# The head of a gated S4 and feed-forward kernel: the order of the first requests, the root of block 0, and two sums cut differently

## The chip, the cores and the metric

The kernel runs on one core of one Trainium2 chip. The metric is device time in microseconds (us) of one execution; the median of three runs of the kernel before is 442.58 us. All arithmetic is in float32.

## The reference

The input `x` has 2 x 1024 rows of 512 numbers. Cut to what matters:

```python
xn = layernorm(x)                                   # over the 512 numbers of a row, eps 1e-5
s  = causal_convolution(xn, K) + D * xn             # K: a kernel of length 512 from an S4 state space
h1 = xn @ w1.T + 2 * (xn @ A1.T) @ B1.T             # w1, w3: 1376 x 512, LoRA rank 16
h3 = xn @ w3.T + 2 * (xn @ A3.T) @ B3.T
g  = silu(h1) * h3
y  = g @ w2.T + 2 * (g @ A2.T) @ B2.T               # w2: 512 x 1376
out = x + s * silu(y)
```

## The kernel before

**Tiling.** The 2048 rows are four blocks of 512 rows (0 to 3), each of four tiles of 128 rows. Blocks 0 and 1 form the first superblock, 2 and 3 the second. The 1376 hidden units are five pairs of 128-wide chunks and a last chunk of 96, for `w1` and for `w3`. The LoRA terms are merged into the weights on the chip: a product of rank 16 on TensorE (PE), then `merge` adds twice that to the weight tile on VectorE (DVE, line 393).

**Products.** The two big products use Strassen's scheme in Winograd's form, with seven products and some sums of operands in place of eight products. It is applied twice for the pairs: an outer level over rows (b11, b21, b12, b22) and weights, an inner level within these. So each pair has seven chains (1, 2, 6, 7, 5, 3, 4), one for each outer product, and each chain has seven steps, one for each inner product. The last chunk has one chain for each superblock. A step is a product into a PSUM bank on PE (line 756) and often a copy of that bank by ScalarE (ACT: lines 776, 794) or an addition by DVE (lines 780, 870) that frees the bank. The PSUM has two banks for each of the tags x, y, w and aux; `bank(tag)` takes the next of a tag, `bank(tag, True)` borrows it without moving on.

**Sums of operands.** `outer_token_sum` (L328) and `inner_token_sum` (L341 for name 3, L343 for name 2, L345 for 4, L347 for 1) make the token sums, `outer_weight_sums` (L441) and `inner_weight_sum` (L453) those of the weights, all on DVE. An inner token sum is made for the raw tokens (`xr`, three parts of 512 columns, `raw` true) and for the outer sums (`xt`, four parts), as one instruction or two. GpSimd (POOL) takes over some additions (L870) and the product of the gate (L837), after which SP stores the result to `g_dram` (L808).

**Head.** `load_x` requests a block's tiles. Block 0 comes over the SP and the ACT queue; block 1 goes to single tiles; blocks 2 and 3 to free room in `t_in`. The DMA requests of SP and ACT share eight semaphores in turn, so each request waits until the one eight places before it has landed. Each block is normalized: statistics (`norm_stats`, L247 and L248, on DVE), the reciprocal root (`norm_root`: L281, `rsqrt` with L57 to L66, then L284), the normalization itself (`normalize`: ACT L293, POOL L297), and the transposition by PE (L304), whose result ACT copies (L312; for blocks 1 and 3 L314 and L315). Block 3's statistics are made by ACT (L254, L265). `keep_warm` gives PE idle products (L991) while it waits for data.

**LoRA groups.** The rank-16 factors lie in rows 0 to 15 of each quarter of the partitions: groups 0 and 1 hold those of `w1` and `w3`, groups 2 and 3 a second copy of both. `lora_last` uses groups 0 and 1. `merge_pair`, used for pair 0, makes the product of half a pair from groups 0 and 1, and is called twice; `merge_whole_pair`, used for pairs 1 to 4, uses all four groups at once and gives four merges.

**Order.** PE, DVE, ACT and POOL run in the order in which the program emits instructions. That order is set by hand: `at(place, what)` puts a piece of work at a number, pieces are emitted in rising order of these numbers, and `after(delay, what)` adds one at a distance from the piece that is being emitted. A chain's step is placed by tables such as `PLACES`; one step of a pair's chain is worth about one unit. The code up to `pair_chain` runs first, then the places from -11 on. SP takes the requests as they are emitted.

Of the kernel before, what the change touches and what calls it, by code (L numbers as in the profile page):

```python
# [49 lines left out]
def rsqrt(nc, pool, v, shape):  # L50


    y = pool.tile(shape, F32, tag="rs_y", name="rs_y")
    t = pool.tile(shape, F32, tag="rs_t", name="rs_t")
    part = 3.0 / 8.0
    c2 = part * 0.703952253
    nc.vector.tensor_scalar(  # L57
        y.bitcast(I32), v.bitcast(I32), -0.5, float(0x5F1FFFF9), ALU.mult, ALU.add
    )
    nc.vector.tensor_tensor(t, y, y, ALU.mult)  # L60
    nc.vector.scalar_tensor_tensor(t, t, -c2, v, ALU.mult, ALU.mult)
    nc.vector.scalar_tensor_tensor(y, t, c2 * 2.38924456, y, ALU.add, ALU.mult)
    nc.vector.tensor_tensor(t, y, y, ALU.mult)
    nc.vector.scalar_tensor_tensor(t, t, 1.0 / part**2, v, ALU.mult, ALU.mult)
    nc.vector.scalar_tensor_tensor(t, t, -10.0 / 3.0, t, ALU.add, ALU.mult)
    nc.vector.scalar_tensor_tensor(y, t, 5.0, y, ALU.add, ALU.mult)  # L66
    return y
# [40 lines left out]
def s4_gated_ffn(  # L108
# [59 lines left out]
    def bank(tag, borrow=False):  # L168

        i = turn[tag]  # L170
        if not borrow:
            turn[tag] = 1 - i
        return psum.tile([P, 512], F32, tag=f"{tag}{i}", name=tag, bufs=1)
# [36 lines left out]
    def value(tag="s"):  # L210
        return upool.tile([P, TB], F32, tag=tag, name=tag, bufs={"s": 10, "c": 4}[tag])
# [4 lines left out]
    def at(place, what):  # L216
        heapq.heappush(events, (place, next(count), what))

    def after(delay, what):
        at(now[0] + delay, what)  # L220
# [2 lines left out]


    def load_x(b):
        room = (None, None, t_in[4], t_in[6])[b]
        tiles = []
        for tt in range(NTT):
            t = value() if room is None else room[:, tt, :]
            queue = nc.scalar if b == 0 and tt % 2 else nc.sync  # L230
            queue.dma_start(out=t, in_=x[bass.ds(b * TB + tt * P, P), :])
            tiles.append(t)
        return tiles

    norms, sums_of_x = {}, {}

# [38 lines left out]
            norms[b][:, :, 1], sums_of_x[b][:, 2, :], 1.0 / DIM, None, mult  # L275
        )

    def norm_root(mv, *blocks):
        n = len(blocks) * NTT
        veps = small.tile([P, n], F32, tag="veps", name="veps")  # L280
        nc.vector.tensor_scalar(veps, mv[:, :, 1], EPS, None, add)  # L281
        rstd = rsqrt(nc, small, veps, [P, n])
        shift = small.tile([P, n], F32, tag="shift", name="shift")
        nc.vector.scalar_tensor_tensor(shift, mv[:, :, 0], -1.0, rstd, mult, mult)  # L284
        for n, b in enumerate(blocks):
            norms[b] = [t[:, n * NTT : (n + 1) * NTT] for t in (rstd, shift)]
# [9 lines left out]
            else:  # L296
                nc.gpsimd.tensor_scalar(t, t, rstd[:, one], shift[:, one], mult, add)  # L297

    def transpose(b, tiles, tag="aux"):
        sb, low = divmod(b, 2)  # L300
        for tt in tiles:
            ps = bank(tag)
            for dc in range(NDC):
                nc.tensor.transpose(  # L304
                    ps[:, dc * P : (dc + 1) * P],
                    x_in[b][tt][:, dc * P : (dc + 1) * P],
                    ident,
                )
            at_ = slice(tt * P, (tt + 1) * P)
            halves = ps.rearrange("p (c k t) -> p c k t", c=2, k=2)  # L310
            if low == 0:
                nc.scalar.copy(xr[:, 0:2, sb, :, at_], halves)  # L312
            else:
                nc.scalar.copy(b12[sb][:, :, at_], halves[:, 0])  # L314
                nc.scalar.copy(xr[:, 2, sb, :, at_], halves[:, 1])  # L315
# [18 lines left out]

    def inner_token_sum(name, raw, half=None):
        src, lo, n = (xr, 0, 3) if raw else (xt, 3, 4)
        some = slice(n) if half is None else slice(2 * half, 2 * half + 2)
        to = {i: t[:, lo : lo + n, :][:, some] for i, t in t_in.items()}
        b11, b21, b12_, b22 = (src[:, some, s, k, :] for s in range(2) for k in range(2))
        if name == 3:  # L340
            nc.vector.tensor_tensor(to[7], b22, b12_, sub)  # L341
        elif name == 2:
            nc.vector.tensor_tensor(to[6], to[7], b11, add)  # L343
        elif name == 4:
            nc.vector.tensor_tensor(to[4], b21, to[6], sub)  # L345
        else:
            nc.vector.tensor_tensor(b12_, b12_, b11, sub)  # L347
# [21 lines left out]
    def load_lora(queue, group, d, h, lo, hi):  # L369
        rows = slice(32 * group, 32 * group + R)  # L370
        if d is not None:
            queue.dma_start(out=lora["d"][rows, :], in_=d)
        queue.dma_start(out=lora["h"][rows, : hi - lo], in_=h[:, lo:hi])
        lora["base"][group] = lo
# [6 lines left out]
    def lora_product(ps, group, dc, lo, n, start=True):  # L381
        d, h = lora_factors(group, lo, n)
        nc.tensor.matmul(
            ps,
            lhsT=d[:, dc * P : (dc + 1) * P],
            rhs=h,
            start=start,
            stop=True,
            skip_group_check=True,
        )  # L390

    def merge(to, ps):
        nc.vector.scalar_tensor_tensor(to, ps, LORA_SCALE, to, mult, add)
# [11 lines left out]
                )  # L405
        return w

    def merge_pair(c, w, half, tag="aux"):

        ps = [bank(tag), bank(tag)]  # L410
        for k in range(2):
            for v in range(2):
                n = slice(k * 2 * P, (k + 1) * 2 * P)
                lora_product(ps[v][:, n], v, 2 * half + k, PAIR_AT[c], 2 * P, k == 0)
        for v in range(2):
            to = w[:, (1, 2, 0, 3)[2 * v + half]].rearrange("p k m h -> p (k m h)")
            after(1.6 + v, lambda to=to, v=v: merge(to, ps[v]))

    def merge_whole_pair(c, w, first=None, delays=(1.15, 2.3, 4.3, 4.4)):

        ps = [first or [bank("y", True), bank("w", True)], [bank("aux"), bank("aux")]]
# [41 lines left out]
    def load_last():  # L463
        both = const.tile([P, 2, 2 * NDC * LASTR], F32, tag="w2b", name="last")
        w, s = (
            both[:, i].rearrange("p (a b h) -> p a b h", a=n, h=LASTR)
            for i, n in enumerate((2, 4))
        )
        for v, src in enumerate((w1T, w3T)):
            nc.sync.dma_start(  # L470
                out=w[:, v], in_=src[:, LAST * P :].rearrange("(dc p) h -> p dc h", p=P)
            )
        return w, s

    def lora_last():
        ps = [bank("y"), bank("y")]
# [487 lines left out]

    x_in = {0: load_x(0)}
    warm = const.tile([P, 1], F32, name="warm")
    nc.gpsimd.memset(warm, 0.0)
    make_identity(nc, ident)
    lora_tiles(LSPLIT)
    factors = (a1, b1T), (a3, b3T)  # L970
    for v, f in enumerate(factors):
        load_lora((nc.sync, nc.scalar)[v], v, *f, LSPLIT, HID)
    nc.scalar.activation(warm, warm, AF.Silu)
    x_in[1] = load_x(1)
    make_upper_triangular(nc, tri, 1.0, diag=True)
    w_last, s_last = load_last()
    w_pair, s_pair = {0: load_pair(0)}, {c: {} for c in range(NPAIR)}
    x_in[2], x_in[3] = load_x(2), load_x(3)
    w_pair[1] = load_pair(1)
    for v, f in enumerate(factors):  # L980
        load_lora(nc.sync, 2 + v, *f, LSPLIT, HID)

    def other_factors():
        for v, (_, h) in enumerate(factors):
# [18 lines left out]
    ps_last = lora_last()  # L1003
    mv = norm_tile(0)
    norm_stats(0, range(NTT))
    norm_root(mv, 0)
    normalize(0)

    keep_warm(primed[1], 4)
    transpose(0, range(NTT))  # L1010
    mv = norm_tile(1)
    norm_stats(1, range(2))
    merge_last(w_last, ps_last, 0)
    norm_stats(1, range(2, NTT))
    norm_root(mv, 1)
    merge_last(w_last, ps_last, 1)
    mv_late = norm_tile(2, 3)
    ab_last = last_operands(w_last, s_last)

# [37 lines left out]
            add_chain(2 + 7 * c + n, pair_chain(c, n), places)  # L1057
    at(-10, lambda: normalize(1))
    at(-9.9, lambda: last_sums(w_last, s_last))
    at(-9, lambda: merge_pair(0, w_pair[0], 0))  # L1060
    at(-3.8, lambda: merge_pair(0, w_pair[0], 1))
    for i in range(2):
        at(-6 + i, lambda i=i: transpose(1, range(2 * i, 2 * i + 2), "y"))
    for n, name in enumerate((3, 2, 1)):
        at((-2.3, -1.5, -0.45)[n], lambda name=name: outer_token_sum(0, name))
        at(-0.6 + 0.3 * n, lambda name=name: outer_weight_sums(w_pair[0], (name,)))
    at(0.4, lambda: outer_token_sum(0, 4))
    at(0.8, lambda: outer_weight_sums(w_pair[0], (4,)))
    for tt in range(NTT):
        at(-6 + 0.8 * tt, lambda tt=tt: norm_stats(2, (tt,)))  # L1070
        at(-1.4 + 0.1 * tt, lambda tt=tt: act_sums(3, tt))
        at((-0.3, -0.2, 1.7, 1.8)[tt], lambda tt=tt: act_squares(3, tt))
    at(-0.9, lambda: act_means(3))
    at(1.9, lambda: act_variances(3))
    at(6.9, lambda: norm_root(mv_late, 2, 3))
    at(7.3, lambda: normalize(2))
    at(7.7, lambda: normalize(3, (0,)))
    for n, place in enumerate((12.1, 12.8, 13.7, 14.4)):
        b, i = divmod(n, 2)
        at(place, lambda b=b, i=i: transpose(2 + b, range(2 * i, 2 * i + 2)))  # L1080
# [5 lines left out]
        at(when, lambda name=name: inner_weight_sum(w_pair[0], s_pair[0], name))  # L1086
    for name, raw, when, *half in (
        (3, True, 21.6),
        (2, True, 22.8),
        (3, False, 24.2),  # L1090
        (2, False, 30.2),
        (1, True, 34.4),
        (1, False, 37.5, 0),
        (1, False, 40.3, 1),
        (4, True, 47.6),
        (4, False, 50.2, 0),
        (4, False, 52.3, 1),
    ):
        at(when, lambda of=(name, raw, *half): inner_token_sum(*of))
# [495 lines left out]
```

## Time and profile before

| | |
|---|---|
| median of three runs | 442.58 us (442.12, 442.58, 443.27) |
| the profiled execution | 442.84 us |
| its span, first to last instruction | 441.0 us |
| granted clock of PE | 0.998 of full speed |
| busy: PE, DVE, POOL, ACT | 434.3, 317.6, 207.9, 144.3 us |
| moved by DMA | 53.61 MB, mean 122 GB/s |

The page gives the busy time of each engine and the chain that ended last; other views list the same execution by stretches or in order of time. In a line of the timeline the columns are start and duration in us, engine, line of the kernel, operation, output<-inputs by tile name, shapes, and count; a bracket gives the idle time of the engine before it and what ended that. PE is the product, PEld the load of its weights. The time of a run is longer than the span by what lies around the first and the last instruction (here 1.8 us).

### The profile page before, as it was taken

How to read it: one execution, taken by the hardware profiler on the slowest of the kernel's cores; microseconds unless marked ns; L12 is line 12 of the kernel's file. 1: busy time of each engine (PE TensorE's matmuls, PEld its weight loads, DVE VectorE, ACT ScalarE, POOL GpSimd, SP SyncE). 2: the span in 40 equal slices, each digit the busy share in tenths (PEclk: the TensorE clock that was granted, in tenths of full speed). 3: DMA queues.
4: the chain of work that ended last, by engine and by line, in shares of the span. 5: the costliest groups of instructions: out<-in, count | busy, mean ns of one | idle time of the engine just before them, and what ended most of it. 6: DMA issues, size and time to landing. Idle time of an engine off the chain costs nothing.

```text
span 441.0 us, 5158 instructions
## 1 busy us (share of the span) xinstructions
PE 434.3 (98%) x1704; PEld 269.1 (61%) x1704; DVE 317.6 (72%) x536; ACT 144.3 (33%) x296; POOL 207.9 (47%) x156
## 2 busy tenths in 40 slices
PE   7999999999999999999999999999999999999996
PEld 7645334344444444444443446888898999999996
DVE  5899999954974687469745796979786885653234
ACT  2777242453255324532453242211101212212221
POOL 1416468895689368946894468400000122222221
PEclk9999999999999999999999999999999999999999
DMA  8931304025102500250035526395901832422211
GB/s 242 364 83 44 124 0 149 10 84 159 36 24 80 159 24 25 88 170 25 25 129 206 162 94 214 94 364 189 344 33 71 296 129 95 144 97 95 77 67 48
DMA packets 35467, 53.61 MB, mean 122 GB/s; under 512 B 4689, under 2 KB 21521, under 8 KB 35313
## 3 DMA queue, kind: packets, MB, share of 16 engines
q1 hardware_dynamic: 35088, 52.69, 36.3%
q10 hardware_dynamic: 352, 0.60, 0.4%
q8 instruction: 13, 0.21, 0.2%
q14 instruction: 14, 0.11, 0.1%
HBM read 33.88 MB, written 19.40 MB: 121 GB/s over the span
## 4 chain that ended last, share of the span: by engine, by line
PE 86%; DVE 7%; DMA 2%; ACT 2%; issue 1%; POOL 0%; SPq 0%; DVEq 0%; ACTq 0%; POOLq 0%
PE x L756 43%; PE y L756 22%; PE w L756 11%; PE aux L930 4%; PE w L930 2%; DMA s<-in_x_dram 1%; DVE xt L328 1%; DVE s L453 1%; DVE w L441 1%; DMA w<-in_w1T_dram 1%; PE y L529 1%; PE aux L711 1%; DVE t_in L343 1%; ACT c L254 1%; DVE aux L1310 1%
## 5 line engine op out<-in xcount | busy, mean ns | idle before, releaser
L1313 POOL TENSOR_TENSOR o<-o,xin 128x512 f32<-128x512 f32 (+1 forms) x17 | 23.3, 1369 | 133.0 <-DVE o L1312 133.0
L837 POOL TENSOR_TENSOR s<-c,s 128x512 f32<-128x512 f32 (+1 forms) x44 | 63.2, 1442 | 17.6 <-ACT c L829 12.4
L776 ACT COPY s<-x 128x512 f32<-128x512 f32 (+1 forms) x54 | 31.5, 584 | 84.5 <-PE x L756 84.4
L756 PE MATMUL x<-t_in,s 128*128 128x512 f32 (+1 forms) x148 | 55.4, 501 | 0.0
L870 POOL TENSOR_TENSOR s<-ua_three,s 128x512 f32<-128x512 f32 x20 | 35.9, 1793 | 25.4 <-DVE s L780 25.4
L780 DVE TENSOR_TENSOR s<-s,y 128x512 f32<-128x512 f32 (+1 forms) x54 | 36.0, 679 | 15.7 <-PE y L756 10.6
L756 PEld LDWEIGHTS x<-t_in,s 128*128 128x128 f32 x148 | 26.6, 190 | 23.3 <-issue 11.7
L870 POOL TENSOR_TENSOR ua_three<-ua_three,s 128x512 f32<-128x512 f32 x20 | 30.6, 1529 | 13.8 <-DVE s L780 13.8
L756 PE MATMUL y<-t_in,s 128*128 128x256 f32 (+1 forms) x108 | 35.9, 459 | 0.1
L1335 ACT COPY z<-x 128x256 f32<-128x256 f32 x24 | 8.8, 371 | 70.5 <-PE x L756 70.4
L870 POOL TENSOR_TENSOR s<-u_three,s 128x512 f32<-128x512 f32 x20 | 29.4, 1474 | 1.8 <-ACT c L829 1.0
L1310 DVE TENSOR_TENSOR aux<-aux,m 128x384 f32<-128x384 f32 x32 | 18.1, 565 | 15.8 <-PE aux L930 14.3
L829 ACT ACTIVATE c<-c 128x512 f32<-128x512 f32 x40 | 25.2, 632 | 12.9 <-DVE c L870 12.9
L756 PEld LDWEIGHTS y<-t_in,s 128*128 128x128 f32 x108 | 20.1, 190 | 11.6 <-issue 8.1
L794 ACT COPY w<-x 128x512 f32<-128x512 f32 (+1 forms) x37 | 21.1, 570 | 11.6 <-PE x L756 11.5
L870 POOL TENSOR_TENSOR u_three<-ua_three,u_three 128x512 f32<-128x512 f32 x10 | 15.6, 1556 | 13.4 <-DVE u_three L780 13.3
L756 PE MATMUL x<-t_in,w 128*128 128x512 f32 x40 | 21.0, 605 | 0.0
L756 PE MATMUL x<-xt,w 128*128 128x512 f32 x40 | 20.7, 598 | 0.0
L756 PE MATMUL x<-xr,w 128*128 128x512 f32 x40 | 20.6, 614 | 0.0
L756 PE MATMUL x<-xr,s 128*128 128x512 f32 x40 | 20.5, 614 | 0.0
L756 PE MATMUL x<-xt,s 128*128 128x512 f32 x40 | 20.4, 592 | 0.0
L756 PE MATMUL y<-xt,w 128*128 128x512 f32 x40 | 19.8, 592 | 0.0
(302 smaller groups left out, 908.7 us busy)
## 6 DMA issues: line engine op xcount, KB each, us to landing
g_dram<-s SPq DMA_DIRECT2D x40, 256.0 KB, 2.1
g<-g_dram SPq DMA_DIRECT2D x10, 512.0 KB, 5.8
xin<-in_x_dram SPq DMA_DIRECT2D x16, 256.0 KB, 2.7
out_dram<-o SPq DMA_DIRECT2D x14, 256.0 KB, 2.0
t_in<-g_dram SPq DMA_DIRECT2D x6, 512.0 KB, 4.1
w<-in_w1T_dram SPq DMA_DIRECT2D x10, 256.0 KB, 3.6
w<-in_w3T_dram SPq DMA_DIRECT2D x10, 256.0 KB, 4.9
t_in<-in_x_dram SPq DMA_DIRECT2D x8, 256.0 KB, 5.7
```

The source lines that it names most:

```text
L254: nc.scalar.activation(value("c"), x_in[b][tt], AF.Copy, accum_out=sums_of_x[b][:, 0, tt : tt + 1])
L756: nc.tensor.matmul(ps[:, cols], lhsT=lhsT, rhs=rhs if parts == 1 else rhs[:, cols], start=first and i == 0 and part == 0, stop=i == len(pa ...
L776: nc.scalar.copy(t, self.x)
L780: nc.vector.tensor_tensor(t, t, self.y, add)
L794: nc.scalar.copy(self.w, self.x)
L829: nc.scalar.activation(c, c if src is None else src, AF.Silu)
L837: nc.gpsimd.tensor_tensor(g, act, g, mult)
L870: (nc.vector if o < 20 else nc.gpsimd).tensor_tensor(to, a, b, add)
L930: nc.tensor.matmul(to[:, n * P : (n + 1) * P], lhsT=x_, rhs=by, start=start, stop=True, skip_group_check=True,)
L1310: nc.vector.tensor_tensor(y[:, P:], y[:, P:], m[:, n * P : (n + 3) * P], add)
L1313: (nc.vector if last else nc.gpsimd).tensor_tensor(o, o, self.xin[h][:, cols], add)
L1335: nc.scalar.copy(t, xb)
```

## The change

- Block 1 is loaded into `t_in[7]` by two requests of 512 KB in place of four of 256 KB; blocks 2 and 3 likewise into their rooms.
- The second copy of the LoRA factors (groups 2 and 3) is requested right after the weights of the last chunk, ahead of pair 0, blocks 2 and 3 and pair 1; before, it came behind them. The weights of the last chunk are now requested ahead of the POOL work on `tri`.
- Block 0's reciprocal root: ACT takes the root (`Sqrt`), DVE the reciprocal and one step of refinement. The first activation loads the table for Sqrt; a second warm-up activation after block 0's transposes loads the one for Silu.
- Block 0's transposes use the banks aux, aux, x, aux; block 1's use x (borrowed) and y, y, y. One warm-up product of PE less.
- Pair 0's LoRA is made by `merge_whole_pair`, once, with the banks y, y, aux, aux, and its four merges stand together; `merge_pair` is gone. The second merge of the last chunk moves ahead of block 1's root.
- The statistics of three tiles of block 2 move from -5.2, -4.4 and -3.6 to 0.84, 0.85 and 0.9; its normalization from 7.3 to 7.7.
- The inner token sum of name 2 (T2) is made in four instructions in place of two.

```diff
     def load_x(b):
...
+        if b == 0:
+            tiles = [value() for _ in range(NTT)]
+            for tt, t in enumerate(tiles):
+                (nc.sync, nc.scalar)[tt % 2].dma_start(out=t, in_=x[bass.ds(tt * P, P), :])
+            return tiles
+        room = (None, t_in[7], t_in[4], t_in[6])[b]
+        for tt in range(0, NTT, 2):
+            nc.sync.dma_start(
+                out=room[:, tt : tt + 2, :],
+                in_=x[bass.ds(b * TB + tt * P, 2 * P), :].rearrange("(n p) d -> p n d", p=P),
+            )
+        return [room[:, tt, :] for tt in range(NTT)]
...
+    def refined(mv, veps):
+
+        shape = list(veps.shape)
+        y = small.tile(shape, F32, tag="rs_y", name="rs_y")
+        t = small.tile(shape, F32, tag="rs_t", name="rs_t")
+        root = small.tile(shape, F32, tag="root", name="root", bufs=1)
+        nc.scalar.activation(root, mv[:, :, 1], AF.Sqrt, bias=eps)
+        nc.vector.tensor_scalar(veps, mv[:, :, 1], EPS, None, add)
+        nc.vector.reciprocal(y, root)
+        nc.vector.tensor_tensor(t, y, y, mult)
+        nc.vector.scalar_tensor_tensor(t, t, -0.5, veps, mult, mult)
+        nc.vector.scalar_tensor_tensor(y, t, 1.5, y, add, mult)
+        return y
...
+        if on_act:
+            rstd = refined(mv, veps)
+        else:
+            nc.vector.tensor_scalar(veps, mv[:, :, 1], EPS, None, add)
+            rstd = rsqrt(nc, small, veps, [P, n])
...
-        some = slice(n) if half is None else slice(2 * half, 2 * half + 2)
+        some = slice(n) if half is None else slice(2 * half, min(2 * half + 2, n))
...
-    nc.scalar.activation(warm, warm, AF.Silu)
+    nc.scalar.activation(warm, warm, AF.Sqrt)
     x_in[1] = load_x(1)
+    w_last, s_last, load_of_last = load_last()
+    for v in range(2):
+        load_of_last(v)
     make_upper_triangular(nc, tri, 1.0, diag=True)
-    w_last, s_last = load_last()
+    for v, f in enumerate(factors):
+        load_lora(nc.sync, 2 + v, *f, LSPLIT, HID)
     w_pair, s_pair = {0: load_pair(0)}, {c: {} for c in range(NPAIR)}
     x_in[2], x_in[3] = load_x(2), load_x(3)
     w_pair[1] = load_pair(1)
-    for v, f in enumerate(factors):
-        load_lora(nc.sync, 2 + v, *f, LSPLIT, HID)
...
-    norm_root(mv, 0)
+    norm_root(mv, 0, on_act=True)
     normalize(0)
 
-    keep_warm(primed[1], 4)
-    transpose(0, range(NTT))
+    keep_warm(primed[1], 3)
+    for tt, tag in enumerate(("aux", "aux", "x", "aux")):
+        transpose(0, (tt,), tag)
+    nc.scalar.activation(warm, warm, AF.Silu)
     mv = norm_tile(1)
     norm_stats(1, range(2))
     merge_last(w_last, ps_last, 0)
     norm_stats(1, range(2, NTT))
+    merge_last(w_last, ps_last, 1)
     norm_root(mv, 1)
-    merge_last(w_last, ps_last, 1)
...
-    at(-9, lambda: merge_pair(0, w_pair[0], 0))
-    at(-3.8, lambda: merge_pair(0, w_pair[0], 1))
-    for i in range(2):
-        at(-6 + i, lambda i=i: transpose(1, range(2 * i, 2 * i + 2), "y"))
+    at(
+        -9,
+        lambda: merge_whole_pair(
+            0, w_pair[0], [bank("y"), bank("y")], (1.6, 1.7, 1.8, 1.9)
+        ),
+    )
+    at(-6, lambda: transpose(1, (0,), "x", True))
+    at(-5.9, lambda: transpose(1, range(1, NTT), "y"))
...
-        at(-6 + 0.8 * tt, lambda tt=tt: norm_stats(2, (tt,)))
+        at((-6, 0.84, 0.85, 0.9)[tt], lambda tt=tt: norm_stats(2, (tt,)))
...
-    at(7.3, lambda: normalize(2))
-    at(7.7, lambda: normalize(3, (0,)))
+    at(7.7, lambda: normalize(2))
+    at(7.75, lambda: normalize(3, (0,)))
...
         (3, True, 21.6),
-        (2, True, 22.8),
+        (2, True, 22.8, 0),
         (3, False, 24.2),
-        (2, False, 30.2),
+        (2, False, 30.2, 0),
+        (2, False, 30.3, 1),
+        (2, True, 31.1, 1),
         (1, True, 34.4),
```

More of the change, by code (lines that the diff above doesn't have):

```diff
@@ L225, in load_x @@
     def load_x(b):
[L226 to L233, printed above, removed]
+        if b == 0:
[10 more added lines that the diff above has]
+        return [room[:, tt, :] for tt in range(NTT)]
     norms, sums_of_x = {}, {}
@@ L276, in act_variances, with norm_root @@
         )
-    def norm_root(mv, *blocks):
+    def refined(mv, veps):
[10 more added lines that the diff above has]
+        return y
+    def norm_root(mv, *blocks, on_act=False):
         n = len(blocks) * NTT
         veps = small.tile([P, n], F32, tag="veps", name="veps")
-        nc.vector.tensor_scalar(veps, mv[:, :, 1], EPS, None, add)
-        rstd = rsqrt(nc, small, veps, [P, n])
+        if on_act:
[3 more added lines that the diff above has]
+            rstd = rsqrt(nc, small, veps, [P, n])
         shift = small.tile([P, n], F32, tag="shift", name="shift")
@@ L297, in normalize, with transpose @@
                 nc.gpsimd.tensor_scalar(t, t, rstd[:, one], shift[:, one], mult, add)
-    def transpose(b, tiles, tag="aux"):
+    def transpose(b, tiles, tag="aux", borrow=False):
         sb, low = divmod(b, 2)
         for tt in tiles:
-            ps = bank(tag)
+            ps = bank(tag, borrow)
             for dc in range(NDC):
@@ L406, in load_pair @@
         return w
[L408 to L417, printed above, removed]
     def merge_whole_pair(c, w, first=None, delays=(1.15, 2.3, 4.3, 4.4)):
@@ L468, in load_last, with load @@
         )
-        for v, src in enumerate((w1T, w3T)):
+        def load(v):
             nc.sync.dma_start(
-                out=w[:, v], in_=src[:, LAST * P :].rearrange("(dc p) h -> p dc h", p=P)
+                out=w[:, v],
+                in_=(w1T, w3T)[v][:, LAST * P :].rearrange("(dc p) h -> p dc h", p=P),
             )
-        return w, s
+        return w, s, load
     def lora_last():
@@ L966, in s4_gated_ffn @@
     warm = const.tile([P, 1], F32, name="warm")
-    nc.gpsimd.memset(warm, 0.0)
+    eps = const.tile([P, 1], F32, name="eps")
+    for t, v in ((warm, 0.0), (eps, EPS)):
+        nc.gpsimd.memset(t, v)
     make_identity(nc, ident)
```

## The prediction

> **What bounds the kernel now.** I read the chain that ended last first, its shares by engine:
>
> ```profile
> PE 86%; DVE 7%; DMA 2%; ACT 2%; issue 1%; POOL 0%; SPq 0%; DVEq 0%; ACTq 0%; POOLq 0%
> ```
>
> PE carries 86% of the chain, and followed in order of time its other pieces lie in the first 62 us, but for single spots. So I took the stretches of 10 us (columns: length, then busy PE, PEld, DVE, ACT and POOL, granted clock, DMA share, GB/s):
>
> ```profile
> 20.00:30.00 10.00, 10.00 (x33) 4.31 (x32) 9.33 (x17) 8.92 (x25) 1.06 (x3) 1.00 0.52 157
> 50.00:60.00 10.00, 9.94 (x24) 3.61 (x23) 9.90 (x9) 3.25 (x6) 4.91 (x2) 1.00 0.00 0
> 70.00:80.00 10.00, 10.00 (x25) 4.24 (x24) 9.97 (x11) 3.82 (x7) 7.56 (x5) 1.00 0.41 126
> 90.00:100.00 10.00, 10.00 (x24) 4.23 (x24) 4.66 (x7) 5.04 (x9) 9.69 (x8) 1.00 0.24 79
> ```
>
> PE and DVE are both full from 20 to 90 us; only after 90 has DVE room (4.66 of 10). An earlier start of PE is therefore worth what DVE, equally full, can follow. The timeline shows where the two meet:
>
> ```profile
> 8.17 0.17 DVE L281 TENSOR_SCALAR veps<-mv 128x4 f32<-128x4 f32 x1
> 10.14 1.52 ACT L293 ACTIVATE s<-s,shift,rs_y 128x512 f32<-128x512 f32 x2 [6.07 <-DVE shift L284]
> 12.34 1.21 PE L304 MATMUL aux<-ident,s 128*128 128x128 f32 x8 [0.24 <-ACT xr L312]
> 15.37 0.56 ACT L794 COPY w<-x 96x512 f32<-96x512 f32 x1 [1.19 <-PE x L756]
> 21.47 1.13 PE L383 MATMUL aux<-lo_h,lo_d 16*128 16x256 f32 x8
> 21.55 1.29 DVE L328 TENSOR_TENSOR xt<-xr,b 128x512 f32<-128x512 f32 x2 [0.64 <-ACT xr L315]
> ...
> 52.79 2.64 DVE L343 TENSOR_TENSOR t_in<-t_in,xr 128x1536 f32<-128x1536 f32 x1
> 55.35 0.67 DVE L870 TENSOR_TENSOR c<-ua_one,x 128x512 f32<-128x512 f32 x1
> 69.31 2.95 DVE L347 TENSOR_TENSOR xt<-xt 128x1024 f32<-128x1024 f32 x1
> 81.91 0.68 DVE L870 TENSOR_TENSOR c<-u_one,x 128x512 f32<-128x512 f32 x1
> 82.64 0.30 PEld L756 LDWEIGHTS x<-t_in,w 128*128 128x128 f32 x2 [0.75 <-DVE c L870]
> ```
>
> Until 21.5 us a chain of small steps sets the pace. DVE's last long wait is the 0.64 before 21.55; from there it runs almost without a break to 92, and PE waits for it at 56 (behind the row of 55.35) and at 82.64 (behind that of 81.91).
>
> **Root from Sqrt.** Removed is DVE's row of ten small instructions (L281, L57 to L66, L284), 8.17 to 10.11. In its place stand Sqrt on ACT, then reciprocal, three small operations and the shift; veps runs beside Sqrt. The last statistics end at 8.13. Two hand-overs of 0.04; Sqrt of 128x4 by its nearest row, the 128x1 ACTIVATE at 3.88 us, 0.20; reciprocal 0.18 (128x4, L669); four more at the 0.196 spacing of L57 to L66: 9.4, or 0.7 earlier. At 0.8 for Sqrt (L293, 128x512 with pointer operands) only 0.1 earlier.
>
> **Transposes in a third bank.** The wait at 12.34 (0.4 with its refill) goes, and ACT copies four tiles in a row at 0.48 (L312). Its two normalizations last from 9.4 to 10.95, the copies to 13.0 instead of 14.2. The warm-up matmul less ran while PE waited anyway: nothing.
>
> **Second table load.** After the copies ACT loads the table for Silu. The load at 2.58 us took 1.28, the ACTIVATE behind it 0.20: ACT is taken to 14.5, and behind it waits the copy L794 that opens the last chunk's second product; it goes at 14.55 (before: 15.37). The LoRA products hide this, just: PE has them from 14.0 to 15.1, then needs the copy. Without that cover it costs 0.4. The Trainium skill, "ScalarE: Activation LUTs", section "What ACT_TABLE_LOAD costs", adds about 1.38 us of drain to every switch of the table. The load in this trace shows none (its ACTIVATE follows 0.01 later); by the page the copy would go at 15.9, and the sum below would be 0.4 slower instead of 0.4 faster.
>
> **LoRA four at a time.** Before, two sets of L383 stand in PE's row, 1.06 each (15.26 and 21.47); four row groups together took 1.08 at 30.48. PE is relieved of 1.06. On DVE four merges (L393, 0.60 each) stand together behind the root of block 1, where two did: those of 22.76 and 24.56 come forward. The first two banks are those of the last chunk's LoRA, so PE also waits for the second L393 on `last`, which now stands ahead of block 1's root and delays it by its 0.6. DVE starts block 1's statistics 0.7 earlier, waits some 0.4 for the first `last` piece, and ends the root near 15.9 as now (15.78).
>
> **Factors and block 1.** The moved factor requests pass the first pair, blocks 2 and 3 and the second pair on SP. SP's thirteenth to sixteenth requests went out at 7.43 to 9.02; these are now the factors. The two `last` transfers took 3.7 and 4.7 us, landing near 11.1 and 12.6; DMA is full there (share 1.02 to 1.08), so sending them 1 us earlier brings nothing, and the factors follow at some 0.2 each: 13.4. PE asks at 14.0. High end: 9.02 and the longest landing of lo_d, 6.4, give 15.4. The first pair lands 0.7 later, near 16.3; DVE's merges run from 15.9 to 18.3, so they wait little. Blocks 2 and 3 land 0.7 later too; their statistics come later than before, and ACT's sums have over 1 us of room. Block 1 in two requests moves the same bytes: nothing, 0.3 either way.
>
> **Sum to 21 us.** The last chunk's second product goes at 15.15 instead of 16.32; block 1's transposes at 16.9 instead of 18.11 (normalized at 16.8, so no earlier). Over three banks only the fourth tile waits, 0.6 for ACT. The last copy is done at 20.1 instead of 21.5: DVE's L328 starts 1.35 earlier, and PE, one LoRA set lighter, is 1.6 earlier.
>
> **What DVE makes of it.** From L328 on it is 1.35 earlier; two merges gone, 1.2 more; three tiles' statistics of block 2 (L247 with L248, 0.80 each) now stand behind the sums, 2.4 back; waits of 0.11 and 0.24 (30.1, 34.2) close, as ACT is ahead. That leaves 0.5 at the merges of 34.8. **T2 in four parts** (L343): the row of 52.79 becomes two thirds, 0.53 less (L341: 2.28 for 2048, 1.74 for 1536), so DVE is 1.0 ahead at 55.35. The row of 59.34 becomes two halves, 0.06 more, and PE's next product needs only the first. The last third costs 0.60 some 2 us later: 0.4 ahead is left, and at 82 PE waits for DVE as before. The later place of the normalizations (7.7 for 7.3) costs nothing: it lets a ready copy pass the late root. The sum: 0.4 earlier. Against the profiled execution's own 442.84 (span 441.0, 1.8 around it) that is 442.4; the median of the runs, 442.58, is 0.26 lower: **442.2 us**.
>
> **Rivals.** First, *the whole head start survives* (faster). DVE's row from 63 to 76 us holds waits: L347 of 1024 takes 1.69 at 65.89 and 2.95 at 69.31, L345 of the same size 1.21 at 82.51; with the rows of 1536 at 63.15 and 75.28 it is some 3.2 us, always with POOL on SBUF beside it. If the new order meets POOL 1 us less, DVE no longer holds PE; 1.35 to 1.6 remain, and the stalls at 56 and 82 (up to 0.5) may go: 440.5 to 441.2. Second, *the split opens DVE to POOL* (slower): while DVE works back to back on SBUF, POOL's L870 at 48.69 takes 5.12; it gets in at a break, and DVE then loses 0.5 to 1.7 (65.89, 69.31). Four parts for two make two more breaks, 1.0 to 3.4; less the 0.4, 443.2 to 445.6. It decides once DVE loses over 0.4 more between 52 and 74 us. Against it: POOL's work is the same and gets in somewhere anyway. Third, *the factors do not come first*: eight requests stood ahead already and still do (block 0, groups 0 and 1); landing at 15.4, they hold PE 1.4: 443.6.
>
> **How the numbers follow.** Forecast 0.45, first rival 0.33, second 0.14, third 0.08. About 0.3%, 1.3 us, is what a measurement of this kernel can tell from no change; the forecast and the third rival lie within it almost whole, the first rival beyond it, the second mostly. Faster 0.36, same 0.49, slower 0.15. The forecast's own range is 441.3 to 443.0 (Sqrt at its long end, one meeting with POOL more or less); to leave out no more than 2 in 10 it must reach through the first rival and into the second: 440.5 to 443.9.
>
> **What would show it.** Right: normalization at 9.4, the second table load ended by 14.6, one L383 set near 14.0 and none at 21, L328 near 20.2, DVE full from there to 91, and the stall at 82 still behind L870. Wrong: DVE idle before 80 us (first rival), more L343 or L347 rows above 2 us (second), L383 waiting for lo_h after 14.5 (third), or a stall that no row of before has.

## The result, and the profile after

| | before | changed |
|---|---|---|
| median of 20 runs each | 442.16 us (441.69 to 443.27) | 444.49 us (442.62 to 446.57) |
| ratio, 95% interval | | 1.0047 [1.0035, 1.0059] |
| the profiled execution, its span | 442.84, 441.0 | 444.26, 442.5 |

The change makes the kernel slower, by 2.3 us of the median. Two things stand out in the times alone. The changed kernel's runs spread over 4 us, those of before over 1.6. And six of its 20 runs show a granted clock of 0.992 to 0.995 and take 445.5 to 446.6 us; the other fourteen are at 0.997 to 1.000. The profiled execution is none of the six, so this profile shows only a part of the loss.

The chain that ended last, shares by engine (it could be followed back only to 49 us, so they can't be set beside those of before):

```profile
PE 79%; DVE 6%; DMA 2%; issue 0%; ACT 0%; DVEq 0%; SPq 0%
```

The same stretches as before (columns as there):

```profile
20.00:30.00 10.00, 9.31 (x32) 3.64 (x34) 9.29 (x17) 8.96 (x24) 1.16 (x4) 1.00 0.54 191
50.00:60.00 10.00, 9.93 (x24) 3.59 (x23) 9.91 (x10) 2.92 (x6) 5.44 (x2) 1.00 0.00 0
70.00:80.00 10.00, 10.00 (x25) 4.22 (x24) 8.96 (x11) 3.44 (x6) 9.84 (x6) 1.00 0.48 138
90.00:100.00 10.00, 10.00 (x24) 4.07 (x23) 4.95 (x8) 5.60 (x10) 9.69 (x8) 1.00 0.22 79
```

PE now waits in the first stretch, and from 70 to 80 POOL has 2.3 us more (9.84 for 7.56) and DVE 1.0 less: DVE there waits for PE, which had waited for DVE just before. The timeline (lines 328, 343, 347, 383, 453, 756, 794, 837 and 870 of before are now 349, 364, 368, 404, 463, 769, 807, 850 and 883):

```profile
7.42 0.17 DVE L289 TENSOR_SCALAR veps<-mv 128x4 f32<-128x4 f32 x1
7.48 0.30 ACT L288 ACTIVATE root<-mv,eps 128x4 f32<-128x4 f32 x1 [3.40 <-DVE mv L252]
8.81 1.52 ACT L314 ACTIVATE s<-s,shift,rs_y 128x512 f32<-128x512 f32 x2 [1.03 <-DVE shift L305]
11.63 0.56 DVE L414 SCALAR_TENSOR_TENSOR last<-y,last 128x384 f32<-128x384 f32 x1 [0.99 <-DMA last<-in_w1T_dram]
12.44 1.28 ACT L1029 ACT_TABLE_LOAD   x1
13.74 0.20 ACT L1029 ACTIVATE warm<-warm 128x1 f32<-128x1 f32 x1
14.27 0.56 ACT L807 COPY w<-x 96x512 f32<-96x512 f32 x1 [0.33 <-PE x L769]
20.64 1.29 DVE L349 TENSOR_TENSOR xt<-xr,b 128x512 f32<-128x512 f32 x2 [1.29 <-ACT xr L336]
...
61.02 1.08 DVE L463 TENSOR_TENSOR s<-w 128x896 f32<-128x896 f32 x1
62.02 1.76 DVE L364 TENSOR_TENSOR t_in<-t_in,xr 128x512 f32<-128x512 f32 x1
63.70 0.67 DVE L883 TENSOR_TENSOR ua_one<-ua_one,w 128x512 f32<-128x512 f32 x1
64.30 1.74 DVE L368 TENSOR_TENSOR xr<-xr 128x1536 f32<-128x1536 f32 x1
69.51 1.13 PE L769 MATMUL x<-xr,s 128*128 128x512 f32 x2 [0.49 <-DVE ua_one L883]
69.98 1.21 DVE L368 TENSOR_TENSOR xt<-xt 128x1024 f32<-128x1024 f32 x1
74.11 0.69 DVE L883 TENSOR_TENSOR ua_one<-ua_one,w 128x512 f32<-128x512 f32 x1 [1.03 <-PE w L769]
83.28 1.13 PE L769 MATMUL x<-t_in,w 128*128 128x512 f32 x2 [0.54 <-DVE c L883]
238.88 1.12 PE L769 MATMUL y<-t_in,s 128*128 128x512 f32 x2 [0.54 <-DVE w_a L414]
```

The fourth piece of T2 at 62.02 is a sum over 512 columns; free, that takes 0.68 (so in the profile of the kernel with the statistics between the sums, below). It took 1.76, and the next instruction on DVE starts 1.15 later than before. At 69 us DVE is still 0.67 late, and PE waits for it at 69.51. The sum behind, at 69.98, then runs without POOL beside it and takes 1.21, where the one of before took 2.95 at 69.31. DVE would be 1.0 ahead, but now it has to wait 1.03 for PE, at 74.11. Two further sums beside POOL (at 75.31, 2.43 for 2.29, and at 78.26, 1.56 for 1.08) put it behind again, and PE waits a second time at 83.28, where it is 0.64 later than before. Counted from start to start of products, beyond their usual spacing, the two stalls are 0.66 and 0.71. In the kernel before, the stall at this second place is 0.09: the 0.75 in its row of 82.64 is idle time of the weight load, not of PE. The wait at 238.88, 0.54 in its row and 0.70 counted from start to start, is for a merge of `w2` whose transfer landed at 238.04, 1.2 us later than in the profile of before. Such waits come and go: in the profiles of the kernels below the same place shows nothing in ten, and 0.23 to 0.71 in four.

### The profile page after: what moved, and what is told of

Same layout as the page of the kernel before. It is cut to its first block, busy times and chain, and to the rows that moved or that the text cites. A ratio compares the mean times of both kernels' runs of the same rounds, so it can differ in the third digit from the quotient of the medians.

```text
span 442.5 us, 5158 instructions
## 1 busy us (share of the span) xinstructions
PE 433.1 (98%) x1702; PEld 268.1 (61%) x1702; DVE 315.6 (71%) x534; ACT 146.0 (33%) x299; POOL 213.5 (48%) x157
## 4 chain that ended last, share of the span: by engine, by line
PE 79%; DVE 6%; DMA 2%; issue 0%; ACT 0%; DVEq 0%; SPq 0%
PE x L769 40%; PE y L769 21%; PE w L769 10%; PE aux L943 4%; PE w L943 2%; DMA w_a<-in_w2T_dram 2%; DVE t_in L364 1%; DVE t_in L362 1%; PE y L404 1%; PE aux L724 1%; DVE s L793 1%; DVE aux L1335 1%; DVE ua_one L883 0%; DVE xt L349 0%; DVE o L1337 0%; DVE xr L368 0%
## 5 line engine op out<-in xcount | busy, mean ns | idle before, releaser
L850 POOL TENSOR_TENSOR s<-c,s 128x512 f32<-128x512 f32 (+1 forms) x44 | 66.9, 1527 | 14.6 <-ACT c L842 12.2
L883 POOL TENSOR_TENSOR ua_three<-ua_three,s 128x512 f32<-128x512 f32 x20 | 31.1, 1556 | 12.4 <-DVE s L793 12.4
L807 ACT COPY w<-x 128x512 f32<-128x512 f32 (+1 forms) x37 | 21.1, 571 | 10.7 <-PE x L769 10.6
L769 PE MATMUL y<-xt,s 128*128 128x512 f32 x40 | 19.8, 592 | 0.0
```

The source lines that it names most:

```text
L769: nc.tensor.matmul(ps[:, cols], lhsT=lhsT, rhs=rhs if parts == 1 else rhs[:, cols], start=first and i == 0 and part == 0, stop=i == len(pa ...
L807: nc.scalar.copy(self.w, self.x)
L850: nc.gpsimd.tensor_tensor(g, act, g, mult)
L883: (nc.vector if o < 20 else nc.gpsimd).tensor_tensor(to, a, b, add)
```

## The experiments

All are compared with runs of the kernel before on the same chip; the ratio is to these. Theory A: the cut of T2 meets POOL. Theory B: it costs nothing, transfers do. Theory C came from the first four profiles: POOL's small operation L264 is locked out. Theory D: late transfers make the spread.

**T2 again in two** (the changed kernel, `(2, True, 22.8)` and `(2, False, 30.2)` in place of four lines).

> The changed kernel with T2 again in two instructions; all else of the change stays. Theory A (the fourth piece of T2 meets POOL: it took 1.76 us at 62.02 where 0.67 is free, and DVE then reaches the additions that PE waits for at 69.5 and 83.3 late): those two stalls, 0.66 and 0.71 us, fall to 0.1 to 0.2, and the time is 0.6 us below the changed kernel's 444.5, 443.9 or less. Theory B (the cut of T2 costs nothing; what was lost, was lost to transfers such as that of w2, whose landing held PE 0.70 at 238.9): within 0.3 us of 444.5, with a late stall again near 83.

Ratio 1.0031 [1.0013, 1.0049], median 443.95, spread 441.67 to 446.26. The stalls at 69 and 83 are gone, as theory A says, but the profiled execution took 446.26: PE waited 2.67 us at 31.1 (from start to start of products, beyond their spacing; 2.51 as idle time), a stall that neither of the first two profiles has.

**Only T2 in four** (the kernel before with these four lines).

> The kernel before with only T2 in four instructions. Theory A: the fourth piece stands behind the same inner weight sum, near 62.6, POOL gets in there, the piece takes 1.7 us, and PE waits behind DVE at 82 by 0.6 more: 442.8 or more against 442.16 before. Theory B: the two halves relieve DVE at 55 by 0.5 as forecast and the late piece gives it back: within 0.3 us of before.

Ratio 0.9994 [0.9983, 1.0005]; spread 441.76 to 443.28, as narrow as before. The piece took 1.77 and PE waited 0.59 and 0.71 behind it, just as A says, yet the time did not rise: this profile's head was 0.73 earlier by its landings, and the runs can't tell the rest from nothing. What it does show is that the spread comes with the head, not with T2.

**The fourth piece later, and one statistic back in the head** (`31.1` to `34.3`; `(-6, -5.2, 0.84, 0.85)`).

> The changed kernel with the fourth piece of T2 moved from 31.1 to 34.3, so behind the addition L883 that reads PSUM, which then stands at 62.0, where POOL gets in. Theory A: that addition runs in 0.67 beside POOL, the piece behind it loses 0.5 at most, DVE is 0.6 us earlier at 64, PE's stall of 0.66 at 69.5 falls to 0.1: 0.6 below the changed kernel's 444.5. Theory B: within 0.3 us of it.

> The changed kernel with the statistics of the second tile of block 2 back at -5.2, into the 1.29 us that DVE idles ahead of 20.64. DVE's row from 30 to 52 us becomes 0.8 shorter. If DVE's order is what holds PE (theory A), it is up to 0.8 us ahead at 57 and the stalls at 69.5 and 83.3 shrink by as much: 443.7 to 444.2 where POOL is met as often. If DVE's place in the row is not what counts (theory B): within 0.3 of 444.5.

1.0040 [1.0020, 1.0060] and 1.0037 [1.0016, 1.0059], medians 444.32 and 444.61: neither moved the time clear of noise, against theory A's figures. In the first, the piece took 1.16 and the sum behind it 2.82 where 1.74 to 2.23 was usual: the meeting with POOL moved on by one instruction. In the second, the profiled execution again had the wait of 2.67, at 29.6, and a low clock.

The two profiles with that wait gave theory C. ACT's squares of block 3 need the means that POOL makes (L264 and L265, 128x4 each). In the profile of before POOL makes them beside a merge, which reads PSUM:

```profile
24.56 0.68 DVE L393 SCALAR_TENSOR_TENSOR w<-aux,w 128x512 f32<-128x512 f32 x1
24.71 0.22 POOL L260 TENSOR_SCALAR act_sums<-act_sums 128x4 f32<-128x4 f32 x1 [4.98 <-ACT c L254]
24.90 0.22 POOL L261 TENSOR_SCALAR mv<-act_sums 128x4 f32<-128x4 f32 x1
```

The change took both merges out of that row, so DVE runs twelve sums of two SBUF operands back to back. In the changed kernel's profile POOL still got in:

```profile
24.15 0.28 POOL L264 TENSOR_SCALAR act_sums<-act_sums 128x4 f32<-128x4 f32 x1 [4.09 <-ACT c L258]
24.40 0.62 POOL L265 TENSOR_SCALAR mv<-act_sums 128x4 f32<-128x4 f32 x1
```

In the profiles of T2 in two and of the statistic in the head it took 3.59 and 3.38.

**Statistics between the sums** (`(-6, -0.5, -0.35, -0.1)` in place of `(-6, 0.84, 0.85, 0.9)`).

> The changed kernel with the three moved statistics of block 2 set between its outer sums (places -0.5, -0.35, -0.1 in place of 0.84, 0.85, 0.9). Theory C (lock-out: the change took the two merges that read PSUM out of DVE's row of twelve SBUF sums at 20.6 to 27.9; POOL's 128x4 operation L264, for which ACT waits, no longer gets in; it took 3.4 and 3.6 us in the profiles of two experiments, ACT waited 3.0 to 3.2, PE 2.67, and the granted clock fell to 0.50 after that wait): a statistic lets POOL in, as it did at 27.3 and 28.7 there, so L264 takes at most 1.5 us, no wait of PE over 1 us stands before 35, the clock is 0.998 or more, and no run is above 444: median 442 to 443. Theory D (late and uneven landings of blocks 2 and 3 and of later weights make the spread): the runs spread from 442 to 446.5 as before this edit, median 444 to 444.5.

Ratio 1.0011 [0.9999, 1.0023], median 442.85, no run above 444.17 and no clock below 0.998. A statistic reads one SBUF operand, and POOL goes beside it:

```profile
22.99 0.69 DVE L251 BATCH_NORM_STATS2 stats<-t_in 128x6 f32<-128x512 f32 x1
23.48 0.23 POOL L264 TENSOR_SCALAR act_sums<-act_sums 128x4 f32<-128x4 f32 x1 [4.34 <-ACT c L258]
```

Moving the statistics of three tiles takes 1.6 us off (1.0047 to 1.0011, measured in separate series, each against the kernel before), as theory C says and theory D does not.

**Merges between the sums** (delays `(1.6, 1.7, 6.8, 7.8)`), **means on ACT** (L264 and L265 as activations), **the row closed in the kernel before** (second `merge_pair` from -3.8 to -6.3).

> The changed kernel with the last two merges of pair 0 back between the outer sums (-2.2 and -1.2, where they stood before the change; the LoRA product stays one set of four). Theory C: the row has its two PSUM-reading breaks again, near 21.9 and 23.7, and POOL's L264 comes near 24.1 to 24.3: it gets in at the second where ACT is on time, and not where ACT is 0.2 late; fewer runs above 445 than 4 in 12, median 443 to 443.5. Theory D: the same spread and 444 to 444.5.

> The changed kernel with L264 and L265 (the two means of block 3, 128x4) made by ACT itself, so that nothing there waits for POOL; DVE's order stays, ACT has 0.4 us more. Theory C: no run with a clock under 0.998 and none above 444; the median 442.3 to 443.2, since the wait of 2.67 and the half clock can't occur. Theory D: the spread stays, 444 to 444.5.

> The kernel before, with the second LoRA set of pair 0 called at -6.3 in place of -3.8, so that its two merges stand ahead of the row of outer sums and nothing in that row reads PSUM. PE's work is the same; block 1's transposes come up to 1.1 later and PE has 1.1 less behind them: by itself 0 to 0.7 us. Theory C: L260 comes some 3.1 us after the row's start, 0.4 ahead of a sum's end, and is locked out until the row ends, so nearly every run has ACT wait 3 to 4 us, PE over 2 us near 28, and a low clock: median 444.5 to 446.5. Theory D: 442.2 to 443.2.

Means on ACT: 1.0016 [1.0003, 1.0029], 443.03, every clock 0.998 or more: the same cure by another way, with POOL's part removed and DVE's order untouched. This shows that the wait for POOL is the cause of the low clocks and of some 1.4 us of the loss. Its profiled execution, the longest of the twelve at 444.71, loses 1.3 near 301 us, where PE waits for an addition, far behind the head. Merges between: 1.0043 [1.0027, 1.0059]; L264 took 0.23 and no clock was below 0.997, but with two merges more behind the first sums DVE fell back by 2.2 us up to 36 us, and PE waited 1.34 for it at 34.9 (from start to start, beyond the spacing). Theory C was right on the lock-out and its expected time was wrong. Row closed: 1.0014 [1.0003, 1.0025], 443.09, one clock of 0.995 in eleven runs, where C expected a lock-out in nearly all. L260 started 0.46 ahead of the end of a sum there and got in, in 0.63. So a closed row is not enough: when POOL starts counts too.

**ACT half a microsecond later** (the changed kernel with one more activation, its result unused, ahead of block 3's sums).

> The changed kernel with one more 128x512 activation on ACT (0.52 us, its result is not used) ahead of block 3's sums, so that POOL's L264 is released half a microsecond later against DVE's row of sums. Theory C with the phase: started 0.11 or 0.46 ahead of the end of a sum, this operation got in (0.28 and 0.63 us, three profiles); started 0.20 or 0.41 ahead, it was locked out for 3.4 and 3.6 us. 0.11 less 0.52, plus one sum of 0.602, is 0.19: locked out in nearly every run; ACT then waits some 3 us, PE over 2, the clock halves: median 445.3 to 446.5, most runs above 445. Theory D, or if the wait has another cause: 0 to 0.5 above the changed kernel's 444.5, most runs below 445.

Ratio 1.0058 [1.0037, 1.0079], median 445.35; five of six runs at a clock of 0.991 to 0.996, three of them above 445, where most were expected. The timeline, then the stretches:

```profile
25.01 2.78 POOL L264 TENSOR_SCALAR act_sums<-act_sums 128x4 f32<-128x4 f32 x1 [5.42 <-ACT c L258]
27.63 0.69 DVE L251 BATCH_NORM_STATS2 stats<-t_in 128x6 f32<-128x512 f32 x1
27.82 0.72 ACT L269 ACTIVATE c<-t_in,act_sums 128x512 f32<-128x512 f32 x1 [2.44 <-POOL act_sums L264]
29.96 2.69 PE L769 MATMUL x<-xt,last 128*96 128x512 f32 x4 [2.50 <-ACT s L789]
```

```profile
24.00:28.00 4.00, 3.45 (x9) 1.11 (x7) 4.00 (x8) 1.56 (x6) 2.97 (x2) 1.00 0.28 104
28.00:31.00 3.00, 1.04 (x3) 0.54 (x4) 2.01 (x6) 3.00 (x8) 0.00 (x0) 1.00 0.00 0
31.00:34.00 3.00, 3.00 (x15) 1.25 (x17) 1.68 (x10) 1.28 (x4) 0.57 (x2) 0.50 0.00 0
34.00:38.00 4.00, 4.00 (x13) 1.35 (x5) 2.55 (x5) 1.29 (x3) 3.42 (x5) 0.52 0.18 49
```

The whole mechanism lies in these eight lines. POOL's operation waits until DVE's first one-operand instruction at 27.63; ACT waits for POOL, and the copy that PE needs stands behind ACT's squares; PE stands still from about 27.4 to 30; and then its clock is halved (the column after POOL's) for nearly 7 us, while it is busy. The start is 0.21 ahead of the end of a sum (counted to the start of the next), where 0.19 was expected, and it is locked out. That the figure agrees is partly luck: in this execution ACT also waited 0.48 for a tile of block 3, so POOL came 4.62 after the first sum of the row instead of 3.51, about one sum of 0.6 more than the 0.52 that was added. In the changed kernel the start is 0.11 ahead when ACT has run its sums without a break; in the profiles with the lock-out ACT had waited 0.07 to 0.48 for a tile of block 3. That is how a landing a fraction of a microsecond late costs some three: from its first sum to 36 us DVE falls back by 3.3 to 4.3 in these three profiles, by 0.9 in the changed kernel's.

**Statistics between, and T2 in two; and with one statistic in the head; and with the root on DVE** (each on the kernel with the statistics between the sums).

> The kernel with the statistics between the sums (442.85), and T2 in two instructions. Theory A (the fourth piece meets POOL where POOL comes at that moment: 1.68 us in the profiles of the changed kernel and of two others, 0.60 in this one's base): 0.3 to 0.7 below its base, at or below the kernel before. If what is left of the loss does not come from T2: within 0.3 us of 442.85.

> The kernel with the statistics between the sums, of which one tile's goes back to the head (-5.2), where DVE idles 1.1 to 1.3 us ahead of its first sum. If DVE's full row from 20 to 91 sets the pace, the time falls by up to 0.8 (one statistic is 0.80), to 442.0 to 442.5; if PE's or the transfers' pace sets it, it stays at 442.85 within 0.3. Theory C: no clock under 0.997 and no run above 445 either way, since two statistics still stand between the sums.

> The kernel with the statistics between the sums, and block 0's root made by DVE as before the change (no Sqrt, no second table load). By the steps of the forecast the normalization comes 0.7 us later and ACT is free of the load's 1.3; if that lead reaches the end, this is 0.3 to 0.7 slower than 442.85; if DVE's row swallows it, or the freed ACT makes up for it, it is the same within 0.3.

T2 in two: 0.9979 [0.9971, 0.9988], 441.78, faster than before, and twice as far below its base as expected. One in the head: 0.9986 [0.9976, 0.9995], 441.95. Root on DVE: 0.9995 [0.9985, 1.0005], no slower than its base with Sqrt (1.0011, on another chip), where the same or 0.3 to 0.7 slower was expected. The timeline of the first, where the changed kernel has its fourth piece at 62.02:

```profile
60.30 1.08 DVE L463 TENSOR_TENSOR s<-w 128x896 f32<-128x896 f32 x1
61.30 0.67 DVE L883 TENSOR_TENSOR ua_one<-ua_one,w 128x512 f32<-128x512 f32 x1
61.90 2.23 DVE L368 TENSOR_TENSOR xr<-xr 128x1536 f32<-128x1536 f32 x1
```

POOL gets in at the end of L463 in both. Here an addition follows that reads PSUM and runs in 0.67 beside it, and the sum behind loses 0.48 (2.23 for 1.74). In the changed kernel the fourth piece stands there and pays POOL's whole stay, 1.08. DVE's place in five profiles, in us against the profile of before (minus is earlier; the last row is the kernel with both edits, of the next experiment):

| DVE's row in before, at | 21.55 | 36.01 | 55.35 | 62.55 | 81.91 | 90.23 |
|---|---|---|---|---|---|---|
| changed | -0.91 | -0.02 | -0.60 | +1.15 | +0.64 | +0.64 |
| means on ACT | -1.56 | -0.58 | -1.16 | +0.60 | +0.10 | +0.10 |
| statistics between | -1.57 | -0.91 | -1.50 | -0.83 | -0.82 | -0.82 |
| statistics between, T2 in two | -1.87 | -1.20 | -1.25 | -1.25 | -1.24 | -1.24 |
| T2 in two, one statistic in the head | -1.07 | -1.20 | -1.26 | -1.26 | -1.26 | -1.25 |

With T2 uncut, the lead of 36 us goes through to 90 unchanged. With the cut it first grows by 0.6 and then, by 62.55, loses 1.75 (first two rows) or 0.67 (third), by where POOL stands; a part comes back. At 90 the lead is 0.66 to 0.72 less than at 36 in the four profiles with an undisturbed clock in which the fourth piece stands at its place and meets POOL (1.76 or 1.77), and 0.09 to 0.11 less in the three in which it takes 0.68.

**Both edits together, and the same with the root on DVE** (statistics at `(-6, -5.2, -0.35, -0.1)`, T2 in two).

> The changed kernel with T2 in two instructions and the statistics of block 2 at -6, -5.2, -0.35 and -0.1: both single edits together. If DVE's lead at 36 us reaches the end of its row once T2 is uncut (1.25 us from 44 to 95 in the profile of the kernel with the statistics between and T2 in two), the 0.3 to 0.8 that the statistic in the head adds comes on top: 441.0 to 441.6, faster than the kernel before by 0.002 to 0.003. If PE sets the pace by then: 441.8 as without it.

> The same, with block 0's root made by DVE as before the change, no Sqrt and no second table load. Here the row of DVE hands a lead through, so what the Sqrt root is worth must show: 0.7 slower than the kernel beside it by the forecast's step (normalization 9.4 against 10.14), 0.3 to 0.4 if a part of it is lost in ACT's second table load or in the wait for block 1; nothing if the landing of the tiles sets the head.

Both: 0.9966 [0.9953, 0.9979], median 441.19 against 442.71 beside it, the fastest kernel of the study. With the root on DVE: 0.9985 [0.9973, 0.9997], so Sqrt is worth some 0.8 us (0.0019 of 442; the two intervals touch) once the lead can reach the end. Its profiled execution was the longest of its 12 runs and the only one with a clock below 0.998. In it PE had next to nothing to do from 10 to 11, and block 0's transposes then ran at half the clock; in the other profile with the statistics moved and the root on DVE this does not occur. The stretches of 1 us:

```profile
9.00:10.00 1.00, 0.92 (x7) 0.73 (x6) 0.83 (x7) 0.00 (x0) 0.00 (x0) 1.00 1.20 307
10.00:11.00 1.00, 0.10 (x1) 0.10 (x2) 0.96 (x4) 0.96 (x2) 0.90 (x2) 1.00 1.15 229
11.00:12.00 1.00, 1.00 (x7) 1.00 (x8) 0.97 (x4) 0.86 (x2) 0.62 (x1) 0.66 1.10 185
12.00:13.00 1.00, 1.00 (x7) 1.00 (x6) 0.96 (x4) 0.73 (x2) 0.00 (x0) 0.50 1.08 213
```

## Why the prediction was wrong

**The step that failed** is "ACT's sums have over 1 us of room", and with it the pricing of the moved merges by DVE's time alone ("two merges gone, 1.2 more"). ACT's sums had room in time, but the mean behind them goes over POOL, and the two merges were POOL's openings in DVE's row. The three statistics that took their place in the sum, "2.4 back", were priced rightly (from its first sum to 34.8 us DVE loses 0.89, the terms give 0.85) and put one place too late: behind the sums they open nothing, between them they do. This lock-out was on no list of rivals. It accounts for 1.4 to 1.6 us of the median (ratio 1.0047 against 1.0011 with the statistics between and 1.0016 with the means on ACT).

**The last third of T2**, "costs 0.60", was the second mis-sized term: 1.68 in the profile, since POOL met it. The second rival had this mechanism, and DVE lost 1.2 between 52 and 64 us, over its point of 0.4, though it won that back by 72, when PE had already stood still. But it was one break with 1.08 of POOL, not two, and its sign in the text (rows of L343 or L347 above 2 us) would have missed it: the row that shows it is 1.76, for a sum that takes 0.68. Taken out, it gave 0.7 us in the changed kernel (1.0047 to 1.0031), 1.4 with the statistics between (1.0011 to 0.9979) and 0.9 with one of them in the head (0.9986 to 0.9966), the two of a pair measured in separate series; the intervals overlap in the first and the last pair. In the kernel before, the same cut cost nothing measurable; that difference stays open.

**What was right, and one misreading.** Root: from the last statistic to the normalization 2.01 before, 1.43 after, so 0.58 where 0.7 was forecast; this held in all eleven profiles with Sqrt. Copies: the last one is done 3.6 us after the normalization begins, as forecast. The second table load: 1.28, the activation behind it 0.01 later, the copy L807 at 14.27 for 14.55; the drain of 1.38 us of the Trainium skill, "ScalarE: Activation LUTs", "What ACT_TABLE_LOAD costs", shows in none of the profiles, and the measurement decides. One LoRA set at 14.16, none at 21, no wait for its factors: the third rival is out. L349 at 20.64 for 20.2: the first `last` weights landed late in this execution (0.99 of wait at 11.63). From the end of block 0's statistics to the first sum it is 13.42 before, 13.26 here and 12.28 to 12.67 in nine of the other ten profiles with Sqrt (13.49 in the tenth), so the head gives 0.75 to 1.14 in those nine and 0.16 here, for 1.35. "At 82 PE waits for DVE as before" was a misreading: before, PE lost 0.09 there, now 0.71.

**The first rival**, the whole head start survives at 440.5 to 441.2, has the size that the two kernels with T2 uncut and the row opened show: 0.9979 and 0.9966 of 442.16 are 441.2 and 440.7. Its reason was other than the one given: not that POOL is met less, but that a row of DVE in its old order hands a lead through.

The profiled execution itself is 1.5 us longer in span: 0.64 by 83 us (the meeting with POOL), then 0.37 won where before's merge of pair 2 held PE at 106, 0.81 lost at 238.88, and some 0.4 behind 300.

## What to carry to other kernels

Before moving an instruction out of a full row of DVE, ask what it let through, not only what it took: in these traces a PSUM-reading or one-operand instruction between sums of two SBUF operands was the door for POOL, and a POOL operation of 0.2 us can hold ACT, PE and then PE's clock behind it. When runs spread more after a change than before, read the granted clock of each run and profile one of the long ones; the median's profile may not hold the cause. Price a cut by what stands behind the place where POOL gets in, since a sum of two SBUF operands there pays POOL's whole stay (1.08 here).

## What the hardware showed

- POOL's 128x4 operation L264 (L260 in the kernel before) took 0.22 or 0.23 beside a merge or a statistic. Among sums of two SBUF operands it got in, in 0.27 to 0.64, when it started 0.10 to 0.11 or 0.43 to 0.47 us ahead of the end of a sum of 0.6, and was locked out for 2.78 to 3.59, over five or six sums in a row with the one that ran, when it started 0.20 to 0.21 or 0.41 ahead (three profiles). This distance alone does not decide: the like operation L278, also 128x4, got in among such sums when it started 0.17 or 0.29 to 0.31 ahead (five profiles), and missed one at 0.34. What decides stays open. The Trainium skill, "SBUF — State Buffer", "Who interferes with whom", makes it a lock: a DVE instruction with two SBUF inputs and a POOL instruction that reads SBUF exclude each other, the first to start keeps the ports for its whole instruction, and DVE instructions with at most one SBUF input, outside the modes that use both pairs of ports, don't take part. The merges and statistics agree (0.22 or 0.23 beside them), and so does the sum of 0.68 that took 1.76 behind POOL's 1.08.
- In three profiles PE stood still for 2.5 us. Its clock fell to 0.50 at 2.2, 3.5 and 3.9 us after it had stopped (in one 0.3 before the wait was over, in the others 1.0 and 1.4 after it) and stayed there for 3.4 us in one profile and 6.8 in two. In the last kernel PE stood still for 1.0; its clock fell 1.4 after it had stopped, and stayed down for 3.4. The Trainium skill, "TensorE: Matmul & The Clock Gate", "What's actually happening", puts the half rate after an idle window of about 3.4 us; here it followed shorter gaps, and the measurement decides.
